# Layer one's x sums and y joins by accumulating DMAs, with twelve third-level steps in a two-layer Strassen-Winograd kernel

## The chip, the core and the metric

The kernel runs on one core of a Trainium2 chip. The metric is the device time of one execution in microseconds (us), taken as the median of the runs; lower is better. All matrices are float32. The engines are named as in the profile: PE is TensorE's matmul, PEld its weight load, DVE is VectorE, ACT is ScalarE, POOL is GpSimd, and SP is SyncE, which here only issues DMAs.

## What is computed

Two layers act on x of shape (8, 256, 1024), each with a residual. The first is a dense product plus a gated low-rank term whose gates are the softmax of the two best of eight router logits. The second is a dense product with one of 16 weight matrices, chosen by each batch item.

```python
# layer one: W (1024, 1024), Wr (8, 1024), A (8, 16, 1024), B (8, 1024, 16)
base = einsum('btd,od->bto', x, W)
logits = einsum('btd,ed->bte', x, Wr) + 5.0 * one_hot(language_ids, 8)[:, None, :]
topw, topi = top_k(logits, 2)
gates = sum(one_hot(topi, 8) * softmax(topw)[..., None], axis=-2)
h = einsum('btd,erd->bter', x, A)
x = x + base + 2.0 * einsum('bter,bte,eor->bto', h, gates, B)
# layer two: weight (16, 1024, 1024), adapter_ids (8,)
out = x + einsum('bsi,boi->bso', x, weight[adapter_ids])
```

The residuals are folded into the weights: `add_identity` adds the identity matrix to the diagonal blocks of W and of each layer-two matrix.

## The kernel before

**Blocks.** x lies transposed in SBUF as four blocks `xb["11"]` to `xb["22"]`: the first digit halves the 1024 input features, the second the 2048 tokens. Each block is 128 partitions by 4 chunks by 1024 tokens, 2 MB. W lies likewise in `wb`, 1 MB a block, and the result of layer one goes to `yb`, 2 MB a block, each cut into four quarters `y[:, q]` of 128 by 1024 elements. With the temporaries these fill most of SBUF, so the blocks are also scratch: the router weights and the logits lie in y12 at first, and the weights of layer two go later into blocks of x and w.

**Levels.** Layer one is one 2x2 block product by Winograd's form of Strassen's method: seven block products instead of eight, named by keys "1" to "7", whose operands are blocks or sums of blocks. Each block product is again such a product of quarters, whose seven parts are named in the code by PSUM accumulators A, X and B (`product`); the sums s1 to s4 of w and t1 to t4 of x are made by `make_subs` and, for the fourth ones, by `late`. A part is four 128x512 matmuls for its two chunks and two row halves. Some parts are cut once more (`third`): seven matmuls of 128x256 (`piece`) in place of the four, with small sums r and q made on VectorE and four evictions (`take`). Such a step is made for the part called X (the leaf a(0,1) b(1,0), "leaf 2") of products 5, 2, 3 and 4, for the last part of product 4 ("leaf 4"), and for two parts of product 1 ("leaves 3 and 4"): seven steps in all.

**Order.** `opening` runs product 1 while x arrives, mixed with the projections (`project`) of x to the router logits and to h. After it come the rest of the projections, the gates (`gating`, on VectorE), and the transposes of the gated h (`turn`). Then the products follow in the order 5, 2, 6, 3, 7, 4, and then layer two item by item (`adapt`, the items of the second token half first). A product adds its result to a quarter of y when PSUM is evicted (`evict`): onto a base where there is one. The gated low-rank term of B is added inside products 5, 2, 3 and 4 as extra matmuls (L479, `up[rows]` with `hg`).

**Sums and joins on VectorE.** The second level works on sums of blocks that overwrite blocks. The x sums are `x_t1` (x12 becomes x12 - x11, and x22 in the same way, chunk by chunk) and `x_sum`, in four pieces each; the w sums are `w_sum`; at the end of two products the partial result in y21 is added onto y12 and y22 by `join`, quarter by quarter. All of these are VectorE instructions, `tt` at L217.

**Who decides the places.** `tc.manual_schedule()` keeps the order as written. Between the parts of a product, `pump(place)` takes waiting VectorE work from the list `todo`, in order, an equal share of it at each of seven places:

```python
share = sum(t[0] for t in todo) / (last - place + 1)
while i < len(todo) and (share > 0.3 or place == last):
```

TensorE, VectorE, ScalarE and each DMA queue work through their own instructions in order, and wait on semaphores for the data of the others. Weights of layer two are issued on SP's queue by `load_w1`, behind products 6, 3, 7 and 4 for the first two items.

Of the kernel before, what the change touches and what calls it, by code (L numbers as in the profile page):

```python
# [16 lines left out]
P = 128  # L17
# [8 lines left out]
def kernel(  # L26
# [11 lines left out]
):  # L38

# [80 lines left out]
    hT = [flat(yb["11"])[:, j * C * ER : (j + 1) * C * ER].rearrange("p (c e) -> p c e", c=C) for j in range(2)]  # L120
# [52 lines left out]
    load_x(nc.sync, 1, 1, 1, 0, 4)  # L173
    nc.sync.dma_start(b_sb, bT)
    load_w(1, 0)
    load_w(1, 1)
    load_w(0, 1)
# [30 lines left out]
    def use_adapter_ids():  # L208
        nc.vector.tensor_copy(ids_f, ids.rearrange("o t b -> o (t b)"))

        wrap = const.tile([1, NB], F32, name="wrap")
        nc.vector.tensor_scalar(wrap, ids_f[:, NB:], 0.0, float(NAD), ALU.is_lt, ALU.mult)
        nc.vector.tensor_tensor(wrap, ids_f[:, NB:], wrap, ALU.add)
        nc.vector.tensor_scalar(aid_i, wrap, 0.0, float(NAD - 1), ALU.max, ALU.min)

# [63 lines left out]
    def gating(j):  # L279
# [30 lines left out]
        return [(0.23, 0, f) for f in ops] + [(1.22, 0, onto_h)]  # L310

    def turn(j, banks):

        for n in range(C):
            nc.tensor.transpose(banks[n // CQ][:, ts(n % CQ, P)], hT[j][:, n, :], ident)
        for c, ps_g in enumerate(banks):
            nc.scalar.copy(hg[j][:, c, :], ps_g)
# [15 lines left out]
    todo = []  # L333

    def pump(place, last=7):

        share = sum(t[0] for t in todo) / (last - place + 1)
        i = 0
        while i < len(todo) and (share > 0.3 or place == last):
            if todo[i][1] > place:  # L340
                i += 1
                continue
            us, _, fn = todo.pop(i)
            fn()
            share -= us
# [4 lines left out]
    def pieces(fn, out_, x, y, n):  # L350

        w = KH // n
        cut = lambda t, c: t[:, c * w : (c + 1) * w, :]
        return [
            (1.22, 0, lambda c=c: fn(cut(out_, c), cut(x, c), cut(y, c))) for c in range(n)
        ]

    def x_sum(fn, out_, x, y):
        return pieces(fn, xb[out_], xb[x], xb[y], 4)

    def w_sum(fn, out_, x, y):
        return pieces(fn, wb[out_], wb[x], wb[y], 2)
# [4 lines left out]
    def third(key, lhs, rhs):  # L367
# [6 lines left out]
        t, own = {}, {}  # L374

        def op(name, tag, fn, x, y):
            width = P if name[0] == "r" else NQ

            def run():
                t[name] = sub3.tile([P, width], F32, name=f"{name}_{key}", tag=tag)  # L380
                fn(t[name], *(t[v] if isinstance(v, str) else v() for v in (x, y)))

            return us(width), 4, run
# [3 lines left out]
            op("r1", "r13", add, A(1, 0), A(1, 1)),  # L387
            op("q1", "q13", minus, B(0, 1), B(0, 0)),
            op("r2", "r2", minus, "r1", A(0, 0)),
            op("q2", "q2", minus, B(1, 1), "q1"),  # L390
            op("r4", "r4", minus, A(0, 1), "r2"),
            op("q4", "q4", minus, B(1, 0), "q2"),
        ]

        def ops3():
            op("r3", "r13", minus, A(0, 0), A(1, 0))[2]()
            op("q3", "q13", minus, B(1, 1), B(0, 1))[2]()

        def piece(n, acc=None):
            if n in (1, 5):  # L400
                own[n] = single(f"P{n}_{key}", n // 5)[:, n0]
# [9 lines left out]
            nc.tensor.matmul(out_, lhsT=l, rhs=r, start=(n in (1, 5)), stop=True, skip_group_check=True)  # L411

        def take(n, dest, base=None):
# [7 lines left out]
            evict(cut(dest), src, None if base is None else cut(base))  # L421
# [3 lines left out]
    def make_subs(key, w, x, further=True):  # L425

# [8 lines left out]
        def op(name, fn, x, y, first):  # L437
# [3 lines left out]
            def run():  # L441
                t[name] = pool.tile([P, 2, width], F32, name=f"{name}_{key}", tag=name)
                fn(t[name], *(t[v] if isinstance(v, str) else v for v in (x, y)))

            return us(2 * width), first, run

        def late_s():
            minus(t["s2"], a(0, 1), t["s2"])

        def late_t():  # L450
            minus(t["t2"], b(1, 0), t["t2"])

        deep = third(key, lambda: a(0, 1), lambda: b(1, 0)) if further else None
        subs[key] = (a, b, t, (late_s, late_t), deep)
        return [
            op("s1", add, a(1, 0), a(1, 1), 3),
            op("t1", minus, b(0, 1), b(0, 0), 3),
            op("s2", minus, "s1", a(0, 0), 3),
            op("t2", minus, b(1, 1), "t1", 3),
            op("s3", minus, a(0, 0), a(1, 0), 5),  # L460
            op("t3", minus, b(1, 1), b(0, 1), 5),
        ] + (deep[0] if further else [])

    def evict(dest, acc, base=None):

        if base is None:
            nc.scalar.copy(dest, acc)  # L467
        else:
            add(dest, acc, base)

    def multiply(up=None, tokens=None):


        def mm(acc, lhs, rhs, first=False, rows=None, c=0, part=(0, 1), ms=(0, 1)):
# [3 lines left out]
            for i, (l, r, m) in enumerate(steps):  # L478
# [7 lines left out]
                )  # L486

        return mm

    def opening(key, dest):  # L490
# [6 lines left out]
        sums_of = make_subs(key, "11", "11", False)  # L497
# [7 lines left out]
        evict(dest[:, 0], X)  # L505
# [7 lines left out]
        for s in sums_of[:4]:  # L513
            s[2]()
# [6 lines left out]
        evict(dest[:, 3], B)  # L521
        for s in sums_of[4:]:
            s[2]()
        mm(A, t["s2"], t["t2"])
        evict(dest[:, 1], A)
        project(0, 0, None, range(KH, KC), False)
        take(0, 0)
        late[0]()

        ops, ops3, piece, out = third(f"{key}b", lambda: t["s2"], lambda: b(1, 1))  # L530
        for o in ops:
            o[2]()
        late[1]()
        mm(A, t["s3"], t["t3"])
        add(dest[:, 3], A, dest[:, 3])
        quarter = halves(pair("ps_h_1_0", 0))
        chunk = lambda k: project(1, 0, quarter, (k,), k == 0, k == KC - 1)
        chunk(0)
        piece(1)
        out(1, dest[:, 1], dest[:, 1])  # L540
        piece(5)
        ops3()
        chunk(1)
        piece(6)
        out(6, dest[:, 1], dest[:, 1])
        chunk(2)
        b_differences()
# [4 lines left out]
        out(7, dest[:, 1], dest[:, 1])  # L552
        last_out = out
        ops, ops3, piece, out = third(f"{key}a", lambda: a(1, 1), lambda: t["t2"])
        for o in ops[:2]:
            o[2]()
        last_out(5, dest[:, 1], dest[:, 1])
        for o in ops[2:]:
            o[2]()
        add(dest[:, 1], B, dest[:, 1])  # L560
        chunk(4)
        piece(1)
        out(1, dest[:, 2])
        chunk(5)
        piece(5)
        ops3()
        chunk(6)
        piece(6)
        out(6, dest[:, 2])
# [4 lines left out]
        out(7, dest[:, 2])  # L574
        out(5, dest[:, 2], dest[:, 2])
        add(dest[:, 2], A, dest[:, 2])

    def product(key, base, dest, lora=None, tokens=None):
# [4 lines left out]
        old = [base[:, q] if base is not None else None for q in range(4)]  # L583
        A = new("A")
# [3 lines left out]
        if deep is None:  # L588
            pump(1)
            B = new("B")  # L590
            mm(B, t["s1"], t["t1"], True, "1", 1)
            evict(dest[:, 3], B, old[3])
            pump(3)
            mm(A, t["s2"], t["t2"])
            evict(dest[:, 1], A, old[1])
            pump(3)
            mm(X, a(0, 1), b(1, 0), False, "0", 0)
            late[0]()
            late[1]()
            evict(dest[:, 0], X, old[0])  # L600
            pump(4)
            mm(A, t["s3"], t["t3"])
            add(dest[:, 3], A, dest[:, 3])
            pump(5)
            mm(B, t["s2"], b(1, 1), False, "d", 1)
            add(dest[:, 1], B, dest[:, 1])
            pump(6)
            mm(A, a(1, 1), t["t2"], False, "1", 0)
            evict(dest[:, 2], A, old[2])
            pump(7)  # L610
            return
        two = key == "4"
        _, ops3, piece, take = deep
        piece(1)
        take(1, dest[:, 0], old[0])
        pump(1)
        B = new("B")
        mm(B, t["s1"], t["t1"], True, "1", 1, ms=(0,))
        piece(5)
        ops3()  # L620
        mm(A, t["s2"], t["t2"])
        evict(dest[:, 1], A, old[1])
        piece(6)
        take(6, dest[:, 0], old[0])
        late[0]()
        pump(2)
        mm(B, t["s1"], t["t1"], True, "1", 1, ms=(1,))
        evict(dest[:, 3], B, old[3])
        late[1]()
        pump(3)  # L630
        for n in (2, 3, 4):
            piece(n, X)
        mm(X, None, None, False, "0", 0, part=())
        piece(7)
        take(7, dest[:, 0], old[0])
        take(5, dest[:, 0], dest[:, 0])
        if two:
            ops, ops3, piece, take = third(f"{key}b", lambda: a(1, 1), lambda: t["t2"])
            for o in ops:
                o[2]()  # L640
        add(dest[:, 0], X, dest[:, 0])
        pump(4)
        mm(A, t["s3"], t["t3"])
        add(dest[:, 3], A, dest[:, 3])
        if two:
            piece(1)
            take(1, dest[:, 2], old[2])
        pump(5)
        mm(B, t["s2"], b(1, 1), False, "d", 1)
        if two:  # L650
            piece(5)
            ops3()
            piece(6)
            take(6, dest[:, 2], old[2])
# [306 lines left out]
```

## Time and profile before

| | us |
|---|---|
| median of 3 runs | 428.18 (427.34 to 428.52) |
| profiled execution, its own time | 427.97 |
| span of the profile (first to last instruction) | 426.2 |
| PE busy | 421.2 |
| DVE busy | 293.4 |
| ACT busy | 40.0 |
| projections after product 1 | 43.65 to 59.34 of the span |
| products 5, 2, 6, 3, 7, 4 | 59.34 to 230.3 of the span |
| layer two | 230.3 to the end |

The profiled execution is one run; its span is 1.8 us shorter than its time. An engine's busy time is the union of its instructions' durations. The granted TensorE clock is 0.999 of full speed over the span. In the trace one matmul of the code is two MATMUL records, so counts there are doubled. Line numbers such as L479 are those of the kernel before; L479 is the matmul of the second level, L411 that of the third, L245 the projection, L741 layer two, L217 the VectorE addition or subtraction of two tensors.

### The profile page before, as it was taken

To read this page: it belongs to the slowest core of one execution; us is meant where nothing else is said; L and a number is where in the kernel's file an instruction comes from. 1 tells how busy PE (TensorE), PEld (TensorE's weight loads), DVE (VectorE), ACT (ScalarE), POOL (GpSimd) and SP (SyncE) were. 2 spreads that over 40 slices of the span, in tenths; PEclk is the share of its full clock that TensorE was granted. 3 is DMA by queue.
4 is the path that set the end of the run, shared out by engine and by line. 5 is a ranking of instruction groups with operands and counts; after the bars stand their busy time and mean duration, and the time that the engine had idled before them with its cause. 6 is when DMAs were issued, how large, how long until landed. Compare 5 with 4: busy or idle time off the path is not lost.

```text
span 426.2 us, 3410 instructions
## 1 busy us (share of the span) xinstructions
PE 421.2 (99%) x1264; PEld 220.4 (52%) x1264; DVE 293.4 (69%) x409; ACT 40.0 (9%) x67; POOL 2.0 (0%) x10
## 2 busy tenths in 40 slices
PE   8999999999999999999999999999999999999996
PEld 6579975445444454444455444444444444444574
DVE  1646799857999859889598766665747666665531
ACT  2010122020000000000000101010110101010110
POOL 1000000000000000000000000000000000000000
PEclk9999999999999999999999999999999999999999
DMA  8995000000000230720202285565648385550202
GB/s 282 381 399 222 2 0 2 0 0 2 0 0 1 74 125 6 288 100 0 100 0 98 98 282 213 212 214 213 248 173 309 110 288 205 204 192 0 98 2 99
DMA packets 14305, 55.83 MB, mean 131 GB/s; under 512 B 1232, under 2 KB 3536, under 8 KB 9808
## 3 DMA queue, kind: packets, MB, share of 16 engines
q1 hardware_dynamic: 12976, 54.68, 35.7%
q10 hardware_dynamic: 1248, 0.93, 0.7%
q8 instruction: 10, 0.16, 0.2%
q14 instruction: 7, 0.06, 0.0%
q0 software_dynamic: 64, 0.00, 0.0%
HBM read 47.22 MB, written 8.39 MB: 130 GB/s over the span
## 4 chain that ended last, share of the span: by engine, by line
PE 95%; DVE 3%; issue 0%; POOL 0%; ACT 0%; POOLq 0%; DVEq 0%
PE A L741 23%; PE A L479 22%; PE B L741 13%; PE B L479 12%; PE ps_h L245 7%; PE X L741 6%; PE X L479 4%; PE A_last L799 3%; PE P L411 1%; DVE y L217 1%; DVE x L217 1%; PE X L411 1%; PE idle L495 1%; PE A L411 1%; DVE w L217 1%; PE P_1a L411 0%
## 5 line engine op out<-in xcount | busy, mean ns | idle before, releaser
L741 PE MATMUL B<-x,x 128*128 128x512 f32 x128 | 57.5, 592 | 0.0
L479 PE MATMUL A<-t,s 128*128 128x512 f32 x112 | 50.3, 592 | 0.0
L741 PEld LDWEIGHTS B<-x,x 128*128 128x128 f32 x128 | 24.3, 190 | 29.8 <-issue 29.7
L741 PE MATMUL A<-w,x 128*128 128x512 f32 x88 | 39.6, 592 | 0.0
L741 PE MATMUL A<-w,y 128*128 128x512 f32 x88 | 39.1, 592 | 0.0
L217 DVE TENSOR_TENSOR w<-w,w 128x1024 f32<-128x1024 f32 x24 | 28.9, 1221 | 14.0 <-PE A L741 14.0
L245 PEld LDWEIGHTS ps_h<-y,x 128*128 128x128 f32 x256 | 31.7, 190 | 3.3 <-issue 2.9
L479 PEld LDWEIGHTS A<-t,s 128*128 128x128 f32 x112 | 21.2, 190 | 22.9 <-issue 22.5
L245 PE MATMUL ps_h<-y,x 128*128 128x136 f32 x256 | 31.9, 279 | 0.0
L217 DVE TENSOR_TENSOR y<-A,y 128x1024 f32<-128x1024 f32 x19 | 23.2, 1221 | 11.5 <-PE A L479 11.3
L741 PEld LDWEIGHTS A<-w,x 128*128 128x128 f32 x88 | 16.7, 190 | 21.0 <-issue 21.0
L741 PEld LDWEIGHTS A<-w,y 128*128 128x128 f32 x88 | 16.7, 190 | 20.6 <-issue 20.6
L467 ACT COPY z<-A 128x512 f32<-128x512 f32 x21 | 12.3, 586 | 157.9 <-PE A L741 157.9
L479 PE MATMUL B<-t,s 128*128 128x512 f32 x56 | 25.9, 594 | 0.0
L479 PE MATMUL A<-x,w 128*128 128x512 f32 x56 | 25.3, 592 | 0.0
L479 PE MATMUL B<-x,s 128*128 128x512 f32 x48 | 21.6, 592 | 0.0
L217 DVE TENSOR_TENSOR x<-x,x 128x1024 f32<-128x1024 f32 (+1 forms) x20 | 19.3, 1002 | 0.0
L479 PE MATMUL A<-t,w 128*128 128x512 f32 x40 | 18.1, 595 | 0.1
L217 DVE TENSOR_TENSOR y<-B,y 128x1024 f32<-128x1024 f32 x12 | 14.6, 1219 | 5.1 <-PE B L479 5.1
L217 DVE TENSOR_TENSOR z<-X,z 128x512 f32<-128x512 f32 x8 | 5.5, 691 | 17.9 <-PE X L741 15.9
L217 DVE TENSOR_TENSOR t<-x 128x1024 f32<-128x1024 f32 x14 | 17.0, 1217 | 0.3 <-DMA x<-xT_dram 0.3
L217 DVE TENSOR_TENSOR t<-x,t 128x1024 f32<-128x1024 f32 x14 | 17.0, 1217 | 0.0
(166 smaller groups left out, 468.2 us busy)
## 6 DMA issues: line engine op xcount, KB each, us to landing
x<-w_dram SPq DMA_DIRECT2D x24, 1024.0 KB, 4.9
w<-w_dram SPq DMA_DIRECT2D x8, 1024.0 KB, 4.7
out_dram<-z SPq DMA_DIRECT2D x15, 512.0 KB, 3.0
x<-xT_dram SPq DMA_DIRECT2D x6, 1024.0 KB, 13.3
w<-wT_dram SPq DMA_DIRECT2D x3, 1024.0 KB, 15.5
x<-xT_dram SPq DMA_DIRECT2D x4, 256.0 KB, 3.9
x<-xT_dram SPq DMA_DIRECT2D x2, 512.0 KB, 6.8
w<-w11T_dram SPq DMA_DIRECT2D x1, 512.0 KB, 5.6
```

Of the source, the lines that this page charges most:

```text
L217: nc.vector.tensor_tensor(out_, x, y, op)
L245: nc.tensor.matmul(ps[v][:, u * EA : (u + 1) * EA], lhsT=xk(k, j, c)[:, ts(r, P)], rhs=aw_sb[:, k, :], start=(first and k == some[0] and u ...
L411: nc.tensor.matmul(out_, lhsT=l, rhs=r, start=(n in (1, 5)), stop=True, skip_group_check=True)
L467: nc.scalar.copy(dest, acc)
L479: nc.tensor.matmul(acc[:, m, :], lhsT=l, rhs=r, start=(first and i < len(ms)), stop=(i >= len(steps) - len(ms)), skip_group_check=True,)
L495: nc.tensor.matmul(idle[:, 0, :P], lhsT=ident, rhs=ident, start=True, stop=True)
L741: nc.tensor.matmul(accs[name], lhsT=lhs[:, k // 2, k % 2, :], rhs=rhs[:, k, :], start=(first and k == 0), stop=(k == KH - 1), skip_group_c ...
L799: nc.tensor.matmul(acc, lhsT=lhs[:, k // 2, k % 2, :], rhs=rhs[:, k, ts(v, m)], start=(first and k == 0), stop=(k == KH - 1), skip_group_c ...
```

## The change

The x sums and the y joins of layer one are no longer VectorE instructions. They are DMAs issued by GpSimd with `accum_op=ALU.add`, which add the source onto the destination: from SBUF block to SBUF block (`add_x`), from a fresh read of x in HBM (`raw`, a plain load on SP's queue, and `add_raw`, an accumulating one), and from y21 onto y12 and y22 (`join`). Since they only add, sums stand where differences stood, and the signs are turned elsewhere: w sums become differences and the reverse, product 6 subtracts from its base (`sub=True`), the second half of hg is copied with a scale of -1, and in layer two the items of the second token half are evicted with the opposite sign (`neg`). The order of the products is 1, 2, 5, 6, 3, 7, 4. Products 2, 6 and 7 have a third step on leaf 2, product 5 on leaves 2, 3 and 4, products 3 and 4 on leaves 2 and 4, product 1 on two as before: twelve. x11 is not needed after x12 += x11, and its place (`spare`) holds s1 and t1 of products 5, 3 and 4, the r and q of the added third steps, and later the y sums of layer two. The place of waiting VectorE work is found by a small model in the code: a clock for PE and one for DVE, due times of events (`event`), work done ahead when it is free (`ahead`), and work forced before a matmul that needs it (`force`). Layer two keeps `pump`.

```diff
-    hT = [flat(yb["11"])[:, j * C * ER : ...
+    hT = [flat(yb["22"])[:, j * C * ER : ...
...
+    load_w(0, 1)
     nc.sync.dma_start(b_sb, bT)
+    load_w(1, 1)
     load_w(1, 0)
-    load_w(1, 1)
-    load_w(0, 1)
...
+    def copy(out_, x, scale=1.0):
+        if scale == 1.0:
+            nc.scalar.copy(out_, x)
+        else:
+            nc.scalar.activation(out_, x, AF.Copy, scale=scale)
...
+    def ahead(until):
+        while now["dve"] < until:
+            may = [(t, i) for i, t in enumerate(map(free, queue)) if t is not None and t < until]
+            ready = [i for t, i in may if t <= now["dve"]]
+            if ready:
+                t, _, key, fn = queue.pop(ready[0])
+                vec(t, fn, key)
+            elif may:
+                now["dve"] = min(may)[0]
+            else:
+                return
...
+        if 3 in leaves:
+            deep[3] = third(key, 3, lambda: t["s2"], lambda: b(1, 1), 1, (f"{key}:P6",))
+        if 4 in leaves:
+            deep[4] = third(key, 4, lambda: a(1, 1), lambda: t["t2"], 2, (f"{key}:P6",))
...
+        def join(q):
+            if joined is not None:
+                y, x = joined
+                nc.gpsimd.dma_start(y[:, q], x[:, q], accum_op=ALU.add)
+                events[f"{key}:join{q}"] = now["dve"] + 8.0
...
-    def join(y, x):
-        return [(1.22, p, lambda q=q: add(y[:, q], y[:, q], x[:, q])) for q, p in ((0, 4), (3, 5), (1, 6), (2, 7))]
+    def add_x(out_, x, k0=0, k1=KH):
+        nc.gpsimd.dma_start(xb[out_][:, k0:k1], xb[x][:, k0:k1], accum_op=ALU.add)
+    def add_raw(out_, i, j):
+        for c in range(2):
+            nc.gpsimd.dma_start(
+                xb[out_][:, :, c * TQ : (c + 1) * TQ], xT[i, j, c].rearrange("k p n -> p k n"), accum_op=ALU.add
+            )
+    def raw(out_, i, j):
+        for c in range(2):
+            nc.sync.dma_start(xb[out_][:, :, c * TQ : (c + 1) * TQ], xT[i, j, c].rearrange("k p n -> p k n"))
...
     opening("1", y21)
...
+    for k in (0, 2):
+        add_x("12", "11", k, k + 2)
+    event("T1", 17.0)
+    for k in (0, 2):
+        add_x("22", "12", k, k + 2)
+    event("T2", 30.0)
...
+    queue += w_sum(minus, "21", "22", "21", (), "S1")
+    queue += [(2.0, (), "bdiff", b_differences)]
+    queue += make_subs("5", "21", "12", (2, 3, 4), ("T1",), "2", 1)
+    product("2", y21, y11, 0, 0)
+    force(gates)
+    turn(1, singles("ps_g_1"))
+    raw("21", 0, 1)
+    add_raw("21", 1, 1)
+    event("T3", 30.0)
+    queue += w_sum(add, "11", "21", "11", (), "S2")
+    queue += make_subs("6", "11", "22", (2,), ("T2",), "5", 0)
     product("5", None, y22, 1, 1)
-    todo += x_sum(minus, "12", "22", "12")
...
+    raw("12", 1, 1)
+    event("x22", 14.0)
+    queue += w_sum(minus, "12", "11", "12", (), "S4")
+    queue += make_subs("3", "12", "12", (2, 4), ("x22",), "6", 1)
+    product("6", y21, y21, sub=True)
+    add_raw("22", 1, 0)
+    event("T4", 20.0)
+    queue += w_sum(minus, "21", "11", "22", (), "S3")
+    queue += make_subs("7", "21", "21", (2,), ("T3",), "3", 0)
+    product("3", y22, y12, 2, 1, joined=(y12, y21))
+    load_w1(0, "21", "12", "22", "11")
+    event("w0", 18.0)
+    queue += make_subs("4", "22", "22", (2, 4), ("T4",), "7", 1)
+    product("7", y21, y21, joined=(y22, y21))
...
     product("4", y21, y21, 1, 0)
...
+    load_w1(1, "22", "12", "11", "21")
...
+        neg = b >= NB // 2
+        join = minus if neg else add
+        def onto(dest, acc):
+            join(dest, dest, acc)
+        def first(dest, acc):
+            copy(dest, acc, -1.0 if neg else 1.0)
```

Before, the layer-two weights of the first item were loaded behind products 6 and 3, those of the second behind products 7 and 4; after, behind products 3 and 4.

## The prediction

> **What bounds the kernel now.** I read the busy line and the slices of the page first, then a table of windows cut at the products of layer one, then the chain of waits, then the groups by form.
>
> ```profile
> PE 421.2 (99%) x1264; PEld 220.4 (52%) x1264; DVE 293.4 (69%) x409; ACT 40.0 (9%) x67; POOL 2.0 (0%) x10
> PE   8999999999999999999999999999999999999996
> DVE  1646799857999859889598766665747666665531
> DMA  8995000000000230720202285565648385550202
> ...
> q0 software_dynamic: 64, 0.00, 0.0%
> ```
>
> TensorE is busy 421.2 of 426.2 us, and each slice but the first and the last reads 9. The other 5.0 us lie before the first matmul and after the last. Moving waits about can win almost nothing; only less TensorE work can. The DMA engines are idle from about 43 to 145 us. The last line is GpSimd's own DMA queue: 64 packets and no bytes to speak of, so nothing here shows what its transfers cost.
>
> ```profile
> 43.65:59.34 15.69, 15.69 (x137) 15.69 (x136) 13.04 (x34) 2.28 (x6) 0.00 (x0) 1.00 0.00 1
> 59.34:89.80 30.46, 30.46 (x80) 14.78 (x79) 27.25 (x58) 6.10 (x11) 0.00 (x0) 1.00 0.00 1
> 89.80:121.70 31.90, 31.82 (x88) 15.77 (x87) 23.67 (x27) 2.99 (x4) 0.00 (x0) 1.00 0.00 1
> 121.70:145.70 24.00, 24.00 (x58) 10.61 (x57) 22.16 (x26) 1.00 (x1) 0.00 (x0) 1.00 0.00 0
> ```
>
> These windows are the projections and products 5, 2 and 6 (columns: length, then busy PE, PEld, DVE, ACT, POOL, granted clock, DMA share, GB/s). VectorE works 22 to 27 us of each, so it runs close behind TensorE, and it is late once:
>
> ```profile
> 72.82 1.29 PE X L411 x6
> ...
> 76.27 3.43 PE A L479 x8
> ...
> 112.83 2.27 DVE w L217 x2
> 115.10 1.15 DVE y L217
> 116.25 0.04 issue
> 116.29 8.85 PE A L479 x20
> ```
>
> In the chain of waits the last line holds twenty matmul records of 3.43 / 8 = 0.429 us, 8.58 us together, and takes 8.85. It starts when a VectorE addition ends. The four records before it began at 114.33 in the timeline and should have ended at 116.05. So product 2 stalls TensorE by about 0.24 + 0.1 = 0.3 us, the only stall between the opening and the tail. The first two lines give two unit prices, each instruction of the code being two records: a 128x512 matmul is 2 x 0.429 = 0.858 us, a 128x256 one is 1.29 / 3 = 0.430 us. Half the columns cost half the time.
>
> **The TensorE sum.** One third-level step takes the place of four 128x512 matmuls by seven 128x256 ones: 4 x 0.858 - 7 x 0.430 = 0.42 us. The program before has seven such steps (product 1 two, 5, 2 and 3 one each, 4 two). The changed one has twelve (1 two, 2 one, 5 three, 6 one, 3 two, 7 one, 4 two). Five more give 20 x 0.858 - 35 x 0.430 = 2.11 us; the built program has indeed 388 instead of 408 of the large matmuls and 116 instead of 81 of the half ones. The projections, the transposes and layer two are unchanged in number and shape.
>
> **The VectorE sum.** These rows of the groups by form give the prices:
>
> ```profile
> L217 DVE TENSOR_TENSOR x<-x,x 128x1024 f32<-128x1024 f32 x12 | 14.2, 1216 | 0.0
> L217 DVE TENSOR_TENSOR y<-y,y 128x1024 f32<-128x1024 f32 x10 | 12.0, 1220 | 0.1
> L217 DVE TENSOR_TENSOR y<-P,y 128x512 f32<-128x512 f32 x7 | 4.8, 688 | 0.7 <-ACT y L467 0.6
> L217 DVE TENSOR_TENSOR q<-x 128x256 f32<-128x256 f32 x8 | 3.3, 418 | 0.0
> L217 DVE TENSOR_TENSOR r<-w 128x128 f32<-128x128 f32 x8 | 2.3, 286 | 2.0 <-PE P L411 2.0
> ```
>
> By the two orders, VectorE loses 19 additions of 128x1024 (the x sums and y joins go, some evictions take their place) and 4 of 128x512, and gains 20 of 128x128, 28 of 128x256 and 5 of 128x2x256: -19 x 1.22 - 4 x 0.68 + 20 x 0.285 + 28 x 0.42 + 5 x 0.69 = -5 us of 293. It is a swap, not a relief. What changes is its place. I set the rows that stand between two products in the changed order against the TensorE time of each: product 2 about 26 of 31.3 us, product 5 20 of 29.6, product 6 20 of 23.6, product 3 26 of 30.1, product 7 19 of 23.6. None is fuller than the fullest before (22.16 of 24.00), so VectorE does not become the bound. The late addition at 115 us has no counterpart: product 2 now runs first, without the x sums. I count its 0.3 us as won. The tightest place I find is the third step on product 5's P3: its second matmul into the same bank waits for an addition that ends about 12.1 us after P6, and TensorE gets there 12.6 us after P6. Half a microsecond is spare; VectorE 5% slower would use up that.
>
> ScalarE: 18 copies become activations with a scale of the same 128x512 size (0.59 us a copy), one 128x1024 copy less and two of 128x256 more. It is 9% busy; its waits are long except the copy of A to X, and that is unchanged. I cost this at nothing. Signs are turned in the same instructions (an addition becomes a subtraction).
>
> **The DMAs, and the price that no row shows.** Added: four accumulating SBUF to SBUF transfers of 1 MB (x12 += x11, then x22 += x12, in halves), four plain loads and four accumulating loads of 1 MB for x21, x12 and x22, and eight accumulating joins of 0.5 MB. In all 16 accumulating transfers, 12 MB, in GpSimd's queue, which takes them in order.
> The nearest rows are the plain 1 MB ones:
>
> ```profile
> x<-w_dram SPq DMA_DIRECT2D x24, 1024.0 KB, 4.9
> ...
> x<-xT_dram SPq DMA_DIRECT2D x6, 1024.0 KB, 13.3
> ```
>
> 4.9 us is one transfer with little beside it, 13.3 us the median of loads queued behind each other in the opening. The Trainium skill speaks against the accumulating form: "Collectives: The Full Stack", section "The bandwidth ceiling: the fold count and why AG ≠ RS ≠ AR", says that an add in the DMA engine reads two sources through one ring and so runs at half the rate of a copy (ratio 1.93 there). By the row the price is 4.9 us per MB, by the rule an estimate of 2 x 4.9 = 9.8. I take 9.8, and keep 13.3 as the upper end. Now the due times, on the clock of the trace before:
>
> - x12 += x11 may start when the second projection after the opening has read two of x12's chunks: 43.65 + 7.5 + 1.9 = 53. The first sum that needs it stands on VectorE behind product 2's P7 addition, at 59.5 + 20 x 0.858 + 7 x 0.430 + 2 = 82. So 2 MB have 29 us: 14 us per MB.
> - x22 += x12 follows. It is needed by product 6's first sum, which stands among product 5's evictions at about 111. So 4 MB have 58 us: again 14 per MB.
> - The reloads have more: x21 comes free from 74 to 83 and is due at 153, x12 from 107 to 117 and is due at 139 with two plain loads, x22 from 136 to 142 and is due at 178.
> - A join reads y21 that the next product overwrites. Product 7's first join starts some 16 us into it, and product 4 writes that quarter 3.9 us after its start: 23.6 - 16 + 3.9 = 11 us for 0.5 MB. Product 3's first three joins, 1.5 MB, have 22 us.
>
> At 9.8 per MB (4.9 a join) all of these are hidden, and at 13.3 (6.7) only just. At 4.9 they are hidden with half the time to spare, and gain nothing. So the price lies on the path only from about 14 us per MB.
>
> A second rule: "SBUF — State Buffer", section "Who interferes with whom", lets VectorE lock GpSimd out while GpSimd writes the descriptors of such DMAs, for copies and tensor_scalar in the two-port modes, but not for tensor_tensor. The rows above are tensor_tensor; of the other kind the layer has only gating instructions of about 0.2 us. Without the lock I add nothing. With it, each transfer would begin one instruction of 1.2 us later, 1.2 of 29, still hidden. No run here shows it yet.
>
> SP's queue: the reloads stand ahead of the layer-two weight loads, and each waits for a product to end. The first weights can start no sooner than at the end of product 3 (174), four loads of 4.9 us end before 195, and are due at about 200. The second item's stand behind product 4's last use of x22, and are due some 14 us into layer two. HBM carries 8 MB more on engines that idle there: hidden.
>
> **Sum.** 2.11 + 0.3 = 2.4 us less. The profiled execution took 427.97 us with a span of 426.2; it becomes 425.6 with a span of 423.8. It lies 0.2 under the median of the runs, 428.18, so the forecast for the median is 425.8.
>
> **Rivals.**
> 1. The accumulating DMA is slow (slower than before). The place is the sum of x12 in VectorE's queue at 82 and, behind it, product 3's joins. It decides from 14 us per MB. At 16: x22's sum comes 4 x 16 - 58 = 6 us late, of which TensorE sees about 5; the joins add 24 - 22 = 2 and again some 2 at product 4. 9 - 2.4 gives +6.6: 434.8. At 20 it would be far worse. For it: no row of such a transfer, and in-order VectorE carries every eviction behind the wait. Against: twice the plain price is still 4 us short. Chance 0.10.
> 2. The 2.1 us are there but small waits eat half: thin places such as the 0.5 us one, VectorE a tenth slower where GpSimd works beside it, or weights of layer two a little late. Three or four waits of 0.4 us give 425.8 + 1.4 = 427.2. For it: VectorE at 85% in three stages. Against: half-full product 5 recovers. Chance 0.12.
> 3. The change does less than it says: half-wide matmuls cost more than half. The two unit prices exclude that, and the counts are in the program. Not given a chance of its own.
>
> **Numbers.** The main case, 0.78, spans 425.2 to 426.7 (a stall of its own up to 0.6, or prices rounded). A difference of about 0.3%, 1.3 us, is what a measurement of this kernel can tell from none: faster means under 426.9, slower over 429.5. Of rival 2, a small part ends under 426.9, the most within; rival 1 ends slower, but for its mildest part. Faster 0.79, same 0.11, slower 0.10. The range takes in rival 2's 427.2 and leaves out rival 1: 425.1 to 427.4.
>
> **What would show it.** In the profile after: TensorE busy about 419 us; window lengths of 29.6 for product 5 and 23.6 for products 6 and 7; no TensorE wait on VectorE over 0.5 us in layer one; accumulating transfers landing within 10 us per MB. VectorE waits on the software DMA queue, or TensorE waits at the start of product 5, 6, 7 or 4, would prove it wrong.

## The result, and the profile after

The changed kernel takes a median of 425.77 us (425.26 to 426.7, 11 runs); the kernel before, timed in turn with it, 427.63 (427.3 to 428.52, 11 runs). The ratio is 0.9956 [0.9946, 0.9967]: faster by 0.44%, or 1.9 us (1.4 to 2.3 by the interval). The ratios of this document use fast runs alone, which leaves out one execution of the changed kernel when it was run again (2565.31 us) and one with thirteen steps (556.93 us). The profiled execution took 425.69 us with a span of 423.7 us. From the page of the changed kernel:

```profile
PE 418.8 (99%) x1294; PEld 226.1 (53%) x1294; DVE 287.6 (68%) x439; ACT 40.6 (10%) x69; POOL 17.6 (4%) x26
PE   8999999999999999999999999999999999999996
...
DVE  1645699957888989878786666765747666665531
...
DMA  8995089476220964918902384666658385650202
...
q0 software_dynamic: 3904, 12.58, 16.6%
...
PE 99%; POOL 0%; ACT 0%; issue 0%; POOLq 0%
```

TensorE is still the bound and its busy time fell from 421.2 to 418.8. The VectorE links are gone from the chain: its shares were PE 95% and DVE 3%, now PE is 99%. The DMA row is filled where it read zeros, and GpSimd's queue (q0) moved 12.58 MB.

The span is a poor ruler for 2 us, because the opening varies from run to run by up to 1.6 us (first transposes of the gated h at 57.93 to 59.51 in the traces of this study, most of them of kernels with the same code up to there). The ruler below is the stretch from the first of those transposes (ps_g) to the first matmul of layer two (A<-w,y). Layer two itself takes TensorE 192.51 us in every trace (after: 227.75 to 420.26). From the timelines of TensorE, first the kernel before, then after (start, duration, engine, line, what):

```profile
58.47 1.04 PE L315 MATMUL ps_g<-ident,y 128*128 128x128 f32 x8
...
230.17 1.02 PE L741 MATMUL A<-w,y 128*128 128x512 f32 x2
```
```profile
58.38 1.04 PE L326 MATMUL ps_g<-ident,y 128*128 128x128 f32 x8
...
227.75 3.60 PE L863 MATMUL A<-w,y 128*128 128x512 f32 x8
```

The stretch is 230.17 - 58.47 = 171.70 us before and 227.75 - 58.38 = 169.37 after: 2.33 us less. The windows of products 2, 5, 6, 3 and 7 after (length, then busy PE, PEld, DVE, ACT, POOL, clock, DMA share, GB/s):

```profile
59.34:90.90 31.56, 31.56 (x88) 15.75 (x87) 28.79 (x56) 3.44 (x8) 3.00 (x3) 1.00 0.85 180
90.90:120.50 29.60, 29.60 (x91) 16.97 (x90) 19.95 (x41) 5.50 (x11) 1.28 (x1) 1.00 0.47 128
120.50:144.10 23.60, 23.60 (x63) 11.76 (x63) 21.02 (x26) 1.57 (x2) 2.56 (x2) 1.00 0.32 47
144.10:174.20 30.10, 30.10 (x86) 15.98 (x85) 26.27 (x44) 1.00 (x1) 2.61 (x3) 1.00 0.68 177
174.20:197.80 23.60, 23.60 (x64) 11.76 (x63) 19.70 (x28) 1.00 (x1) 3.43 (x4) 1.00 0.55 128
```

PE busy equals the length in each, so no product loses anything that the windows resolve. One line of the chain of waits shows the only gap that I find in layer one:

```profile
120.45 3.50 PE A L551 x8
```

Eight records take 3.434 us elsewhere (0.4292 us each); here 3.50, at the first part of product 6. That is 0.07 us.

The price of the accumulating transfers, which no row of before showed, stands in the DMA issues (count, KB each, median us from issue to landing):

```profile
x<-x POOLq DMA_DIRECT2D x4, 1024.0 KB, 9.9
...
x<-xT_dram POOLq DMA_DIRECT2D x4, 1024.0 KB, 9.3
y<-y POOLq DMA_DIRECT2D x8, 512.0 KB, 5.3
```

And their due time, from the timelines of GpSimd and VectorE:

```profile
53.29 0.91 POOL L973 DMA_DIRECT2D x<-x  x1 [50.49 <-PE ps_h L256]
55.14 0.86 POOL L973 DMA_DIRECT2D x<-x  x1 [0.94 <-PE ps_h L256]
61.20 0.85 POOL L973 DMA_DIRECT2D x<-x  x1 [5.21 <-DMA x<-x]
67.31 0.85 POOL L973 DMA_DIRECT2D x<-x  x1 [5.25 <-DMA x<-x]
```
```profile
82.52 0.69 DVE L228 TENSOR_TENSOR s<-x,w 128x512 f32<-128x512 f32 x1
83.12 1.22 DVE L228 TENSOR_TENSOR t<-x,x 128x1024 f32<-128x1024 f32 x1
```

The first two transfers are x12 += x11, the next two x22 += x12. Each of these waits for the half before it, so the halves of x12 had landed at 61.20 and 67.31. VectorE's first sum that reads x12 starts at 83.12 and waits for nothing: nearly 16 us were spare.

### The profile page after: what moved, and what is told of

Its sections match the earlier page's. It is cut to its first block, busy times and chain, and to the rows that moved or that the text cites. A ratio compares the mean times of both kernels' runs of the same rounds, so it can differ in the third digit from the quotient of the medians.

```text
span 423.7 us, 3569 instructions
## 1 busy us (share of the span) xinstructions
PE 418.8 (99%) x1294; PEld 226.1 (53%) x1294; DVE 287.6 (68%) x439; ACT 40.6 (10%) x69; POOL 17.6 (4%) x26
## 3 DMA queue, kind: packets, MB, share of 16 engines
q0 software_dynamic: 3904, 12.58, 16.6%
## 4 chain that ended last, share of the span: by engine, by line
PE 99%; POOL 0%; ACT 0%; issue 0%; POOLq 0%
PE A L863 23%; PE A L551 21%; PE B L551 13%; PE B L863 13%; PE ps_h L256 7%; PE X L863 6%; PE P L463 5%; PE A_last L930 3%; PE X L551 3%; PE X L463 2%; PE A L463 1%; PE idle L568 1%; PE B L463 1%; PE ps_g L326 0%; ACT z L960 0%
## 5 line engine op out<-in xcount | busy, mean ns | idle before, releaser
L863 PE MATMUL B<-x,x 128*128 128x512 f32 x96 | 43.2, 592 | 0.0
L863 PEld LDWEIGHTS B<-x,x 128*128 128x128 f32 x96 | 18.2, 190 | 22.1 <-issue 22.0
L228 DVE TENSOR_TENSOR y<-P,y 128x512 f32<-128x512 f32 (+1 forms) x31 | 17.6, 567 | 14.0 <-PE P L463 9.1
L228 DVE TENSOR_TENSOR x<-w,x 128x1024 f32<-128x1024 f32 (+1 forms) x11 | 10.6, 968 | 10.8 <-PE A L863 7.8
L225 ACT ACTIVATE z<-A 128x512 f32<-128x512 f32 x12 | 7.2, 597 | 101.4 <-PE A L863 101.4
L228 DVE TENSOR_TENSOR w<-x,w 128x1024 f32<-128x1024 f32 x8 | 9.7, 1225 | 10.2 <-PE A L863 5.7
L551 PEld LDWEIGHTS A<-x,w 128*128 128x128 f32 x56 | 10.3, 190 | 10.8 <-issue 10.5
L228 DVE TENSOR_TENSOR z<-z,X 128x512 f32<-128x512 f32 x7 | 4.8, 687 | 15.9 <-PE X L863 15.9
L551 PE MATMUL B<-t,s 128*128 128x512 f32 x32 | 15.0, 595 | 0.0
L863 PE MATMUL X<-w,y 128*128 128x512 f32 x32 | 14.4, 592 | 0.0
```

Source lines behind the costliest of these rows:

```text
L225: nc.scalar.activation(out_, x, AF.Copy, scale=scale)
L228: nc.vector.tensor_tensor(out_, x, y, op)
L551: nc.tensor.matmul(acc[:, m, :], lhsT=l, rhs=r, start=(first and i < len(ms)), stop=(i >= len(steps) - len(ms)), skip_group_check=True,)
L863: nc.tensor.matmul(accs[name], lhsT=lhs[:, k // 2, k % 2, :], rhs=rhs[:, k, :], start=(first and k == 0), stop=(k == KH - 1), skip_group_c ...
```

## The experiments

Two theories. **A**, the forecast's: the gain is five more third-level steps on TensorE plus the stall of product 2, and the DMAs are hidden work that only makes room on VectorE. **B**: something else of the change matters for TensorE (the transfers themselves, the order, ScalarE's signs), and the steps happen to come out near the difference. Every experiment starts from the changed kernel unless it says otherwise. The changed kernel, run again beside the first experiments on their chip, gave a ratio of 0.9953 [0.9938, 0.9967] and the same stretch of 169.37:

> The changed kernel again, beside its variants on one chip. Theory (TensorE work: five third steps at 0.42 us are 2.1 us, and the 0.3 us stall of product 2 is gone): 2.4 us under the kernel before. Rival (part of it is given back outside the span's TensorE work): nearer the 1.9 us between the medians of the first eleven runs.

By the medians the gain is again 1.9 us (428.23 against 426.37), as the second theory of that expectation has it: of the 2.33 that the stretch loses, the time shows less. Where the rest goes is taken up below.

**Seven steps instead of twelve.** All else stays: DMAs, order, planner.

```diff
-    queue += make_subs("5", "21", "12", (2, 3, 4), ("T1",), "2", 1)
+    queue += make_subs("5", "21", "12", (2,), ("T1",), "2", 1)
-    queue += make_subs("6", "11", "22", (2,), ...
+    queue += make_subs("6", "11", "22", (), ...
-    queue += make_subs("3", "12", "12", (2, 4), ...
+    queue += make_subs("3", "12", "12", (2,), ...
-    queue += make_subs("7", "21", "21", (2,), ...
+    queue += make_subs("7", "21", "21", (), ...
```

> The changed kernel with seven third steps in place of twelve (product 5 on leaf 2 alone, product 6 none, product 3 on leaf 2, product 7 none, product 4 as it is): the steps of the kernel before, with the new DMAs, order and planner. Theory: TensorE does 2.11 us more than in the changed kernel and does not stall, so 2.1 us over it and 0.3 us under the kernel before. Rival (freeing VectorE of the sums is itself worth something, and the steps add little): within 1 us of the changed kernel.

Measured: ratio 0.9998 [0.9989, 1.0008], no gain left. TensorE's timeline:

```profile
57.93 1.04 PE L326 MATMUL ps_g<-ident,y 128*128 128x128 f32 x8
...
229.28 1.88 PE L863 MATMUL A<-w,y 128*128 128x512 f32 x4
```

The stretch is 171.35: 1.98 more than with twelve steps, and 0.35 less than in the kernel before. Five steps are 5 x (8 x 0.4292 - 14 x 0.2158) = 2.06 (0.2158 us is a record of 128x256), less the 0.07 gap, which is gone here too. What is left against before, 0.35, should be the stall, if A is right.

**The stall alone, in the kernel before.** The share of VectorE work that stood ahead of product 2's last evictions is taken one eviction later.

```diff
-        pump(4)
+        if key != "2":
+            pump(4)
...
         add(dest[:, 3], A, dest[:, 3])
+        if key == "2":
+            pump(4)
```

> The kernel before with one call of pump moved in product 2: the waiting VectorE work of place 4 comes behind the eviction of P7 and not in front of it. Theory: the one stall of TensorE in layer one, 0.3 us at 116 us, goes and the time falls by 0.3 us. Rival (the stall is taken up elsewhere, or another addition is late next): no change.

Measured: ratio 0.9985 [0.9976, 0.9994], stretch 171.36, that is 0.34 less than before. The window of product 2 (31.82 busy of 31.90 before):

```profile
89.60:121.20 31.60, 31.60 (x88) 15.91 (x87) 23.37 (x27) 2.99 (x4) 0.00 (x0) 1.00 0.00 1
```

So moving one group of additions gives the stall back without any of the rest, and 171.36 is also what the changed kernel has with seven steps. The two parts of the gain add up: 2.06 + 0.34 - 0.07 = 2.33. To 0.01 us, B has nothing left to explain.

**A thirteenth step**, product 3's third leaf:

```diff
-    queue += make_subs("3", "12", "12", (2, 4), ("x22",), "6", 1)
+    queue += make_subs("3", "12", "12", (2, 3, 4), ("x22",), "6", 1)
```

> The changed kernel with a thirteenth third step, product 3 on leaf 3 too. Theory: TensorE loses another 0.42 us; VectorE gets about 5 us more work in a stage where it works 26.3 of 30.1 us, with product 7's 19.7 of 23.6 behind it, which still fits: 0.4 us under the changed kernel. Rival (VectorE is full there): a wait eats it, 0 to 2 us over the changed kernel.

```profile
58.17 1.04 PE L326 MATMUL ps_g<-ident,y 128*128 128x128 f32 x8
...
227.20 2.74 PE L863 MATMUL A<-w,y 128*128 128x512 f32 x6
```

Measured: stretch 169.03, 0.34 less than with twelve: a step's 0.41 less another gap of 0.07, at 173.4. The ratio to the kernel before is 0.9940 [0.9927, 0.9953], median 425.58. It is the fastest version here by its stretch; its interval overlaps that of twelve steps, so the times alone do not separate the two.

**The same bytes without the addition.** The sixteen transfers copy and do not accumulate; x and y then hold other values.

```diff
-                nc.gpsimd.dma_start(y[:, q], x[:, q], accum_op=ALU.add)
+                nc.gpsimd.dma_start(y[:, q], x[:, q])
...
-        nc.gpsimd.dma_start(xb[out_][:, k0:k1], xb[x][:, k0:k1], accum_op=ALU.add)
+        nc.gpsimd.dma_start(xb[out_][:, k0:k1], xb[x][:, k0:k1])
...
```

`add_raw` is changed in the same way.

> The changed kernel with the sixteen accumulating transfers made plain copies from the same queue, so nothing is added and the values differ. Theory [...]: a 1 MB SBUF to SBUF copy lands in about 5 us against 9.9, and the time does not change. Rival (the price is in GpSimd's issue or in the queue, not in the adding): 8 us or more to landing.

```profile
q0 software_dynamic: 2880, 12.58, 7.7%
```
```profile
x<-x POOLq DMA_DIRECT2D x4, 1024.0 KB, 5.3
x<-xT_dram POOLq DMA_DIRECT2D x4, 1024.0 KB, 5.5
y<-y POOLq DMA_DIRECT2D x8, 512.0 KB, 2.9
```

Measured: ratio 0.9946 [0.9928, 0.9965] and again a stretch of 169.37. The same 12.58 MB take 7.7% of the DMA engines' span instead of 16.6%, and a transfer lands in 5.3, 5.5 and 2.9 us instead of 9.9, 9.3 and 5.3. So with the addition a transfer takes 1.87, 1.7 and 1.8 times as long to land, and none of that reaches the end.

**How slow may they be?** Each half of x12 += x11 is issued twice, then three times (x12 then holds more than the sum).

```diff
-        add_x("12", "11", k, k + 2)
+        for _ in range(2):
+            add_x("12", "11", k, k + 2)
```

> The changed kernel with each half of x12 += x11 issued twice (x12 then holds a different sum). Two of these 1 MB transfers landed in about 14 us together in the changed kernel, so the first half is done at about 53 + 15 + 8 = 76 and the second at 82, against due times of 82 and 84.5. Theory (the price lies on the path only from about 14 us per MB): at the edge, 0 to 2 us over the changed kernel. Rival (VectorE or TensorE already feel the transfers at the single price): 3 us or more over it.

> The changed kernel with each half of x12 += x11 issued three times (x12 then holds a different sum). The halves are done at about 90 and 97. Theory: product 5's first matmul at 90.9 needs the first half, VectorE's queue stands still from 82 with the evictions of product 2 behind it, and the four sums of product 5 can only follow: 12 us over the changed kernel, between 8 and 16. Rival (the wait costs only what the DMA itself is late for product 5's start): under 4 us.

VectorE's timelines, twice and then three times:

```profile
84.89 1.23 DVE L228 TENSOR_TENSOR t<-x,x 128x1024 f32<-128x1024 f32 x1 [1.75 <-DMA x<-x]
```
```profile
98.77 1.23 DVE L228 TENSOR_TENSOR t<-x,x 128x1024 f32<-128x1024 f32 x1 [14.69 <-DMA x<-x]
```

Twice: the queue needs 53.22 to 84.89 for x12, 15.8 us per MB of the sum, and VectorE stands 1.75 us. TensorE does not wait: stretch 169.37, ratio 0.9949 [0.9935, 0.9963]. Three times: 54.17 to 98.77, 22.3 us per MB, and the kernel is slower than before, ratio 1.0236 [1.0219, 1.0254], stretch 181.67 (+12.30). TensorE's timeline, and the windows about its waits:

```profile
98.81 0.75 PE L463 MATMUL P<-x,w 128*128 128x256 f32 x2 [3.72 <-DMA x<-x]
105.67 3.78 PE L551 MATMUL B<-x 128*128 128x512 f32 x4 [6.11 <-DVE y L228]
```
```profile
99.50:105.50 6.00, 0.06 (x1) 0.00 (x0) 6.00 (x11) 1.29 (x2) 3.25 (x3) 0.50 1.05 198
105.50:109.50 4.00, 3.83 (x5) 1.77 (x6) 0.11 (x1) 0.00 (x0) 0.00 (x0) 0.50 1.00 154
109.50:113.00 3.50, 3.50 (x10) 1.77 (x10) 2.13 (x4) 0.00 (x0) 0.00 (x0) 1.00 1.04 191
```

One late transfer becomes two TensorE waits. The first is for the data. The second is for VectorE, which is busy for all 6.00 us of the first window with the additions and evictions that had queued behind its own wait. The clock column reads 0.50 in that window already. A finer cut of the same trace puts the fall between the waits: 1.00 from 98.80 to 99.20, 0.50 from 99.30 to 99.50. It is 1.00 again from 109.60 on. So the first 4 us of matmuls behind the second wait run at half speed and take some 2 us more. That makes 3.7 + 6.1 + 2.0 = 11.8 of the 12.3. Most of the rest is in how a wait is counted: the eight records before the first one start at 91.50 and at 0.4292 us each are through at 94.93, 3.9 us before 98.81.

**The sums back on VectorE, with twelve steps.** First the joins alone (eight additions):

```diff
-                nc.gpsimd.dma_start(y[:, q], x[:, q], accum_op=ALU.add)
+                queue.append((1.22, (f"{key}:ready{q}",), f"{key}:join{q}", lambda: add(y[:, q], y[:, q], x[:, q])))
...
```

> The changed kernel with only the eight y joins on VectorE again; the x sums stay with the DMAs. Products 3 and 7 get 4 x 1.14 = 4.6 us of VectorE work each, beside 26.3 of 30.1 and 19.7 of 23.6 us: 0.8 us too much in the first, 0.7 us of the surplus in the second. Theory (VectorE has some room left even with twelve steps): a small stall, 0 to 1.5 us over the changed kernel. Rival (twelve steps leave no room for any sum): 4 us or more over it.

Measured: stretch 170.36, 0.99 more; from one matmul's start to the next, TensorE loses 0.8 us at 183.6 and 0.2 at 208.8, which is all of it. Ratio to before 0.9972 [0.9960, 0.9984]: less than half of the stretch's gain is lost.

Then x12 and x22 alone (eight additions, ahead of the s sums of products 5 and 6):

```diff
-    for k in (0, 2):
-        add_x("12", "11", k, k + 2)
...
+        return block_sums(add, xb[out_], xb[out_], xb[x], 4, what, name)
...
+    queue += v_sum("12", "11", (), "X1")
...
+    queue += v_sum("22", "12", (), "X2")
...
```

> The changed kernel with only the first two x sums, x12 += x11 and x22 += x12, on VectorE again (eight additions of 128x1024); the other DMAs stay. Product 2's stage, where VectorE works 28.8 of 31.6 us, gets four of them, 4.6 us, product 5's, with 20.0 of 29.6, the other four. Theory (the stage counts, not the total): product 2 stalls by 2 to 3 us and product 5 hardly, 2 to 4 us over the changed kernel. Rival (the total counts, 287.6 of 423.7 us): no change.

Measured: stretch 172.75, 3.38 more, ratio to before 1.0033 [1.0017, 1.0048]: slower than the kernel before, with five more steps in it. Its chain of waits, and its longest wait of TensorE in layer one:

```profile
80.08 1.22 DVE y L228
81.31 1.13 DVE x L228
82.44 2.27 DVE w L228 x2
84.71 0.95 DVE bdiff L228 x2
85.66 0.04 issue
85.70 1.98 PE B L551 x4
```
```profile
PE B L551 <- DVE bdiff L228: 2.2, 1, 2.2
```

It is the pattern that the kernel before had at 115 us: VectorE's queue has grown past what product 2 covers, and TensorE goes on with its B part when VectorE has finished. Of the 5.6 us of VectorE work in the chain TensorE stands for 2.2 (2.5 from matmul to matmul); product 6 loses another 0.7 at 128.6, and product 5 hardly anything (0.1).

Last, all 24 additions (the joins, x12, x22 and both rebuilt blocks; the last two add another block of the same size):

> Twelve third steps, but the x sums and y joins on VectorE again: 24 additions of 128x1024 in place of the accumulating DMAs. For x21 and x22 they add another block of the same size instead of one freshly read from HBM, so the values differ; the amount of work is that of the sums. Theory (the DMAs are what makes room for the added steps): VectorE had 138.5 of 168.7 us from product 2 to product 4 in the changed kernel and gets 24 x 1.14 = 27 us more, 98% full, so TensorE waits at several places: 5 to 20 us over the changed kernel. Rival (VectorE had room and the DMAs matter little): within 1 us of the changed kernel.

Measured: ratio 1.0446 [1.0421, 1.0471], stretch 191.56, 22.2 more, a little over the 20 at which I had ended the range. The busy line of the page, TensorE's longest wait (us in total, times, longest) and two windows:

```profile
PE 426.2 (95%) x1294; PEld 227.4 (51%) x1294; DVE 314.5 (70%) x463; ACT 40.6 (9%) x69; POOL 2.0 (0%) x10
```
```profile
PE P L463 <- DVE y L228: 7.0, 1, 7.0
```
```profile
197.00:204.30 7.30, 0.27 (x2) 0.12 (x1) 7.30 (x10) 0.00 (x0) 0.00 (x0) 0.85 0.47 199
204.30:208.50 4.20, 4.20 (x6) 2.07 (x7) 2.43 (x5) 0.00 (x0) 0.00 (x0) 0.50 0.00 0
```

VectorE is 70% busy over the span and still holds TensorE up for 7.0 us here, since its additions come together at one product's end. The half clock follows again, as it does after another wait of 4.3 us at 152.5: together about 4 us of the 22.2, which my range had not counted. The order of these three kernels was the planner's, with the sums forced ahead of the product that reads them; an order tuned by hand would probably lose less, which was not tried.

## Why the prediction was right

- **Five steps, 2.11 us.** 2.06 by the records, 1.98 with its gap by the run with seven steps.
- **The stall, 0.3 us.** 0.34, shown by removing it alone.
- **Spans.** Predicted 423.8, 425.6 for the profiled execution and 425.8 for the median; measured 423.7, 425.69 and 425.77. That the median fits to 0.03 us is luck: the forecast stood on a median of before of 428.18, from three runs, and in this comparison that is 427.63. The measured gain is 1.9 us, and the 2.4 that was forecast lies just outside its interval of 1.4 to 2.3. Of the stretch's 2.33, 0.2 is given back outside the span, where the changed kernel spends 2.0 us and the kernel before 1.8 (a term that I had left unchanged, and whose cause stays open); the rest is within the opening's scatter.
- **VectorE, 5 us less.** 293.4 to 287.6, 5.8 less. Four of the five rows that I had set were within 1.1 us (20, 20, 26 and 19 against 19.95, 21.02, 26.27 and 19.70). Product 2's was not: 26 forecast, 28.79 measured, in a window that also holds the gates' last small instructions, about 4 us of them. So "none is fuller than the fullest before" held only by a hair (28.79 of 31.56 is 91%, 22.16 of 24.00 is 92%; I had put 83%). The run with x12 and x22 on VectorE shows what that would have cost.
- **The tightest place, 0.5 us spare.** The addition in product 5 ended at 112.80 and TensorE got to the matmul at 114.25: 1.4 spare. Two gaps of 0.07 us were elsewhere (only one of them in the changed kernel), so rival 2, small waits of 1.4 us in all, has a twentieth of its size.
- **The accumulating price, 9.8 us per MB.** Landing takes 9.9 at the median (from HBM 9.3, a join 5.3 against 4.9); single ones of the x sums take 7.4 to 11.6, so "within 10 us per MB" holds for the medians only. The Trainium skill's rule ("Collectives: The Full Stack", section "The bandwidth ceiling: the fold count and why AG ≠ RS ≠ AR") that spoke against the form gives the right price: 1.87 between the two forms here, 1.93 there. That two reads are the reason is shown by no run here. The plain row would have been wrong by half. The step that was mis-sized is what I made of it: two transfers in flight overlap, so x12's 2 MB needed 14 us, 7.0 per MB, and not 19.6. Spare were nearly 16 us where 9.8 per MB leaves 10.
- **Rival 1, its threshold of 14 us per MB.** Its mechanism is real: three times the work gives 438.5, with VectorE's queue standing behind the transfer as described, though TensorE waited for the transfer itself first, 3.7 us. VectorE begins to wait at (83.12 - 53.3) / 2 = 14.9 us per MB, but TensorE only beyond: 15.8 costs it nothing and 22.3 costs 12.3 us. The point lies between. The rival's price left out the half clock. In the changed kernel VectorE waits for no transfer of GpSimd's.
- **The lock rule, nothing.** GpSimd was not held up by additions: a transfer from HBM takes it 1.28 us to issue at 93.67, with no VectorE instruction beside it, and 1.28 at 135.03 and 141.00, beside additions. VectorE was not slowed either: its 128x1024 additions take 1.221 us on average (1.219 before). No instruction of the kind that the rule names stood beside an issue, so the lock itself is untested.

## What to carry to other kernels

Split such a change into what it takes from the bound engine and what only makes room for it: here the steps give 2.06 us and the DMAs nothing by themselves, yet with the x sums back on VectorE the same steps end slower than no change. Work moved to an idle DMA queue needs its landing time against its due time and, for an accumulating one, nearly twice the plain price (1.7 to 1.87 times here). For a few tenths of a microsecond measure a stretch between two fixed instructions, as the opening alone scatters by more.

## What the runs showed of the hardware

- **A long stall of TensorE costs more than its length.** With all sums on VectorE, the next four to seven records after the waits of 4.3 and 7.0 us took up to twice their time (clock 0.50 in the windows), 1.7 and 2.4 us in all. With three transfers it was 2.0 us, and there the clock fell right after the wait of 3.7 us. After the wait of 2.2 us with x12 and x22 on VectorE it stayed at 1.00. Where between 2.2 and 3.7 us the limit lies, these runs do not say.
- **Issue on GpSimd.** A transfer from SBUF to SBUF takes it 0.85 to 0.91 us to issue if it accumulates and 0.53 to 0.56 if it does not; from HBM it is 1.28 to 1.30 and 0.75 to 0.76.
- **Time outside the span.** It is 1.8 us in the kernel before, in its version without the stall, and in those with sums on VectorE or with three transfers; 2.0 in the others with accumulating or plain GpSimd transfers. The number of transfers does not order them so, and the cause stays open.
